# Making a key tile's scores in place from its neighbour's, with the keys' difference, in an attention and mixture-of-experts kernel

## The chip, the cores and the metric

The kernel runs on one core of a Trainium2 chip. The metric is the device time of one execution in microseconds (us); lower is better. A core has TensorE (PE, matmuls), VectorE (DVE), ScalarE (ACT), GpSimd (POOL) and SyncE (SP), each with an instruction queue of its own that it works off in order. They wait for each other by semaphores. Matmuls write into PSUM, which here is eight banks of 128 x 512 float32; the other data lie in SBUF, and DMA queues move data between SBUF and the chip's memory (DRAM).

## The reference

One pre-norm layer on x of 8 x 1024 x 256, float32: `x + attention(layernorm(x))`, then `x + experts(layernorm(x))`. The attention has 16 heads of 16 dimensions and uses one projection for both keys and values:

```python
q, kv = split(x @ Wq), split(x @ Wkv)             # b*H, n, 16
q, kv = rotary(q) * SCALE, rotary(kv)
att = einsum('bmd,bnd->bmn', q, kv)               # 1024 x 1024 per head
out = einsum('bij,bjd->bid', softmax(att), kv)
return out @ Wout + bout
```

The expert part scores every token against 8 experts; each expert takes the 1024 tokens that score highest for it, normalises them, applies a two-layer GELU network, weighs the result and adds it to the tokens' rows.

## The kernel before

**Tiling of the attention.** The work is cut into 32 groups `i`: a batch element b of 8 and four heads. A group has two halves of 512 queries and eight tiles of 128 keys. One *step* handles one key tile for one half and all four heads, so a group has 16 steps and the attention 512. In a step the four heads make two pairs, and for each pair `step_pair` (line 381) issues this on PE:

- `row_max` for the first head (L329): queries times 512 keys into one bank of the pool `ps_m`, and a DVE reduction (L336) to the row's maximum. This runs 13 steps (`LEAD`) ahead of the scores.
- `score_pass` for both heads (L371): the scores, keys on the partitions, into a two-bank tile of the pool `ps_e`. The 64 contraction rows of a head hold its 16 dimensions four times: queries and keys are each split into a high part that fits the matmul's float32r format and a low rest, and the products of all four combinations are summed.
- `score_pass` again for both heads with `last` (L371, `ones_r`): a matmul with ones adds the negative row maxima, which lie in `top_bufs`, to the same tile. So every key tile's scores are finished by two passes per head.
- one exponential on ACT over the pair's 128 x 1024 scores (L397), into SBUF.
- `row_max` for the second head.

After both pairs, every even step issues the value matmuls of the two steps before it (`weigh_values`, L416): their result is copied out of a `ps_m` bank by ACT (L429) and added up on POOL (L431). After every eighth step's maxima, `lay_max` (line 340) combines them on DVE, transposes them on PE and has SP write them to `top_bufs` with eight small DMAs (L363); the first steps of the next half need these.

**Buffers that tie engines together.** `ps_m` has four banks, given out in program order to maxima tiles, value sums, projections, transposes. `ps_e` has two tiles, one for each pair in turn, so each pair gets the same tile in every step. The work pool `side` has two buffers per tag, `prob` six, `kq` three for keys and four for queries.

**Work beside it.** Two kinds of generators are advanced piece by piece between steps by `run_pieces` (line 566): the *prologue* of the next batch element (layer norm, projections L280, rotation on POOL L203 to L206, transposes, splits) and the *epilogue* of the last (output projection L492, two layer norms, gate scores). A piece with much PE work is only taken after an odd step, one per step. In the prologue `split_halves` (line 212) copies a transposed block out of PSUM on ACT as `full` (L222), makes its high part `hi` and its rest `lo` on POOL (L223, L224), and SP writes each to DRAM, twice (L231). Each batch element has eight such calls in four pieces: two halves of its 256 columns, two halves of its tokens, query and key. Groups are loaded from there by `load_keys` and `load_queries` on SP (L304, L315), when the list `loads` (lines 588 to 599) says so: keys of group i from step 16(i-2) on.

**Order.** The tile framework is told to keep the program's order (`manual_schedule`), so each engine's queue is in the order in which these Python functions issue. For the first batch element the prologue runs before the steps, and the first step's maxima follow its loads.

**After the attention** come the selection of each expert's tokens, 30 rounds of bisection on DVE, and the experts' matmuls (from about 1845 us on). The change doesn't touch them.

Of the kernel before, what the change touches and what calls it, by code (L numbers as in the profile page):

```python
# [8 lines left out]
F32 = mybir.dt.float32  # L9
F32R = mybir.dt.float32r  # L10
# [16 lines left out]
def preln_attention_moe_kernel(  # L27
# [50 lines left out]
    with ExitStack() as actx:  # L78
# [132 lines left out]

        def split_halves(b, hf, c, s, pt):

            q_d, k_d = halves[b]
            hi = side.tile([P, QW], F32R, tag="hi", name="hi")
            lo = side.tile([P, QW], F32R, tag="lo", name="lo")
            if b == 0 and c == 0:
                nc.scalar.copy(hi, pt)
                nc.vector.tensor_tensor(lo, pt, hi.bitcast(F32), ALU.subtract)
            else:  # L220
                full = side.tile([P, QW], F32, tag="full", name="full")
                nc.scalar.copy(full, pt)  # L222
                nc.gpsimd.tensor_copy(hi, full)  # L223
                nc.gpsimd.tensor_tensor(lo, full, hi.bitcast(F32), ALU.subtract)  # L224
            rows = slice(c * P, (c + 1) * P)
            for part, src_t in enumerate((hi, lo)):
                if s == 0:
                    dst = q_d[hf, rows, 2 * part : 2 * part + 2, :]
                else:
                    dst = k_d[rows, part::2, hf * QW : (hf + 1) * QW]  # L230
                nc.sync.dma_start(dst, src_t.bitcast(F32).unsqueeze(1).to_broadcast([P, 2, QW]))  # L231
# [8 lines left out]
        def prologue(b):  # L240
# [3 lines left out]
            halves[b] = (q_d, k_d)  # L244
# [5 lines left out]
            qks, xns = [], []  # L250

            def normalised(hf):
                stats = yield from row_stats(xts[hf], "a")
                xn = side.tile([P, T2, D], F32, tag="n", name=f"xn_{b}_{hf}")
                scaled(nc.vector if b == 0 else nc.gpsimd, xn, xts[hf], stats)
                xns.append(xn)
# [3 lines left out]
            for hf in range(2):  # L260
                yield "x"
                xnT = one.tile([P, DC, QW], F32, tag="T", name=f"xnT_{b}_{hf}")
                for c in range(DC):
                    pt = transposed(lambda t: xns[hf][:, t, c * P : (c + 1) * P])
                    nc.scalar.copy(xnT[:, c, :], pt)
# [22 lines left out]
            for c in range(DC):  # L288
                for hf in range(2):
# [3 lines left out]
                    for s in range(2):  # L293
                        pt = transposed(lambda j: qks[hf][:, j, s, c * P : (c + 1) * P])
                        split_halves(b, hf, c, s, pt)
                ready[(b, c)] = True

        def load_keys(i):

            b, g = divmod(i, NG)  # L300
            k = kq.tile([P, 2, N], F32R, tag="k", name=f"k_{i}")
# [6 lines left out]
            grp[i] = {"k": k, "q": []}  # L308

# [58 lines left out]
        def score_pass(i, half, kt, h, last, pt):  # L368
            k, q = grp[i]["k"], grp[i]["q"][half]
# [7 lines left out]
                start=not last,  # L377
                stop=last,
            )

        def step_pair(pair, max_job, exp_job):
# [7 lines left out]
            pt = ps_e.tile([P, 2, QW], F32, tag="e", name="ps_s")  # L389
# [4 lines left out]
            score_pass(*exp_job, e1, True, pt)  # L394
            score_pass(*exp_job, e0, True, pt)
# [168 lines left out]
        ready = {}  # L564
# [22 lines left out]

        loads = []
        for i in range(B * NG):
            needs = (i // NG, i % NG // (NG // DC))  # L590
            loads.append((16 * (i - 2) if i > 2 else -(10**6), needs, load_keys, (i,)))
# [376 lines left out]
```

## Time and profile before

| | |
|---|---|
| median of 3 runs | 2510.09 us (2509.98 to 2511.71) |
| the profiled execution | 2509.83 us, span 2508.1 us |
| mean granted PE clock | 0.946 |
| busy in the span: PE, DVE, ACT, POOL | 2235.2, 1738.8, 1361.3, 1154.8 us |
| steps begin with maxima only / with scores / attention ends | 53 / 87 / about 1845 us |
| DMA | 207.5 MB, mean 83 GB/s |

A profile line of a group of instructions reads: source line, engine, operation, output<-input, shapes, count | busy us, mean ns of one | idle us of that engine just before them, and who ended most of it. A timeline line reads: start us, us, engine, line, operation, tiles, shapes, count of instructions merged, and in brackets the idle time ahead of it with the releaser. In a line of the windows stand a stretch from:to and its length, then busy us (and instructions) of PE, its weight loads, DVE, ACT and POOL, then the granted PE clock (1 is full), the mean busy share of the 16 DMA engines and GB/s. Matmuls on different rows of the array overlap, so the busy times of PE's groups add up to more than its total.

### The profile page before, as it was taken

To read this page: it belongs to the slowest core of one execution; us is meant where nothing else is said; L and a number is where in the kernel's file an instruction comes from. 1 tells how busy PE (TensorE), PEld (TensorE's weight loads), DVE (VectorE), ACT (ScalarE), POOL (GpSimd) and SP (SyncE) were. 2 spreads that over 40 slices of the span, in tenths; PEclk is the share of its full clock that TensorE was granted. 3 is DMA by queue.
4 is the path that set the end of the run, shared out by engine and by line. 5 is a ranking of instruction groups with operands and counts; after the bars stand their busy time and mean duration, and the time that the engine had idled before them with its cause. 6 is when DMAs were issued, how large, how long until landed. Compare 5 with 4: busy or idle time off the path is not lost. (4 is left out here: it accounts for less than half of the span.)

```text
span 2508.1 us, 38250 instructions
## 1 busy us (share of the span) xinstructions
PE 2235.2 (89%) x14228; PEld 1228.0 (49%) x14228; DVE 1738.8 (69%) x3303; ACT 1361.3 (54%) x1723; POOL 1154.8 (46%) x1060
## 2 busy tenths in 40 slices
PE   4999999999999999999999999999952289999998
PEld 2444444445444444444444544445431146666665
DVE  5978878888888788779778878888646843331111
ACT  1477777677677667767766777677720011111111
POOL 3274276456446744654674475344220044443332
PEclk8799999999999999999999999999975589999999
DMA  5215115212331412142142215121030013333321
GB/s 186 92 35 194 61 35 194 68 52 102 128 102 35 177 65 73 69 161 86 52 157 81 75 54 179 52 69 52 27 110 9 1 30 85 74 69 70 77 45 28
DMA packets 127210, 207.50 MB, mean 83 GB/s; under 512 B 13360, under 2 KB 65456, under 8 KB 126896
## 3 DMA queue, kind: packets, MB, share of 16 engines
q1 hardware_dynamic: 113616, 186.39, 21.7%
q0 software_dynamic: 12288, 17.05, 4.1%
q8 instruction: 113, 1.85, 0.3%
q10 hardware_dynamic: 1120, 1.61, 0.2%
q14 instruction: 73, 0.60, 0.1%
HBM read 111.42 MB, written 92.54 MB: 81 GB/s over the span
## 5 line engine op out<-in xcount | busy, mean ns | idle before, releaser
L336 DVE TENSOR_REDUCE nm<-ps_x 128x1 f32<-128x512 f32 x2048 | 1266.9, 681 | 256.7 <-PE ps_x L329 252.2
L397 ACT ACTIVATE e<-ps_s 128x1024 f32<-128x1024 f32 x1024 | 997.0, 1025 | 183.6 <-PE ps_x L329 162.7
L329 PE MATMUL ps_x<-k,q 64*128 64x512 f32 x2048 | 790.6, 435 | 48.3 <-ACT full L222 23.1
L371 PE MATMUL ps_s<-q,k 64*128 64x512 f32 x2048 | 677.8, 432 | 11.4 <-ACT e L397 11.0
L371 PE MATMUL ps_s<-top,ones_r 64*128 64x512 f32 x2048 | 609.6, 394 | 0.0
L329 PEld LDWEIGHTS ps_x<-k,q 64*128 64x128 f32 x2048 | 373.9, 188 | 411.8 <-DVE nm L336 238.2
L416 PE MATMUL ps_av<-e,v 128*32 128x512 f32 x4096 | 504.4, 611 | 16.9 <-DVE nm L336 16.4
L431 POOL TENSOR_TENSOR av<-av,avp 128x512 f32<-128x512 f32 x191 | 244.5, 1280 | 554.9 <-ACT avp L429 554.8
L371 PEld LDWEIGHTS ps_s<-top,ones_r 64*128 64x128 f32 x2048 | 362.3, 187 | 38.0
L371 PEld LDWEIGHTS ps_s<-q,k 64*128 64x128 f32 x2048 | 314.0, 186 | 64.8 <-ACT e L397 47.2
L879 ACT ACTIVATE hT<-ps_h,b 128x512 f32<-128x512 f32 x128 | 88.0, 687 | 369.9 <-PE ps_h L872 369.9
L894 DVE TENSOR_TENSOR o<-ps_o,b2b 128x256 f32<-128x256 f32 x64 | 27.2, 425 | 357.3 <-PE ps_o L886 357.3
L896 POOL DMA_INDIRECT out<-o,idx x64 | 127.4, 1991 | 282.1 <-DMA out<-o,idx 135.2
L416 PEld LDWEIGHTS ps_av<-e,v 128*32 128x32 f32 x4096 | 108.5, 110 | 266.4 <-issue 173.8
L872 PE MATMUL ps_h<-yT,w 128*128 128x512 f32 x512 | 226.4, 600 | 7.7 <-DVE yT L860 7.5
L886 PE MATMUL ps_o<-w,hT 128*128 128x256 f32 x1024 | 223.6, 379 | 0.0
L886 PEld LDWEIGHTS ps_o<-w,hT 128*128 128x128 f32 x1024 | 194.6, 190 | 33.3 <-issue 7.7
L429 ACT COPY avp<-ps_av 128x512 f32<-128x512 f32 x192 | 112.7, 587 | 176.3 <-PE ps_av L416 169.3
L872 PEld LDWEIGHTS ps_h<-yT,w 128*128 128x128 f32 x512 | 96.9, 192 | 125.7 <-issue 109.8
L844 POOL DMA_INDIRECT g<-rows_d,idx x64 | 70.5, 1102 | 148.0 <-DVE ids L819 128.8
L280 PE MATMUL ps_p<-wqkv,xnT 128*128 128x512 f32 x256 | 126.1, 619 | 2.5 <-DVE nm L336 2.2
L203 POOL TENSOR_TENSOR u<-pe,sin 128x256 f32<-128x256 f32 x112 | 79.2, 728 | 84.1 <-ACT pe L197 84.1
(137 smaller groups left out, 1862.8 us busy)
## 6 DMA issues: line engine op xcount, KB each, us to landing
k<-k_d SPq DMA_DIRECT2D x64, 512.0 KB
q<-q_d SPq DMA_DIRECT2D x128, 256.0 KB
q_d<-hi SPq DMA_DIRECT2D x32, 512.0 KB
q_d<-lo SPq DMA_DIRECT2D x32, 512.0 KB
k_d<-hi SPq DMA_DIRECT2D x32, 512.0 KB
k_d<-lo SPq DMA_DIRECT2D x32, 512.0 KB
w<-in_fc_t SPq DMA_DIRECT2D x16, 1024.0 KB
rows_d<-rows SPq DMA_DIRECT2D x16, 528.0 KB
```

What stands on the lines that cost most here:

```text
L280: nc.tensor.matmul(pp, lhsT=xnT[:, c, j * P : (j + 1) * P], rhs=wqkv[:, c].rearrange("p a d -> p (a d)"), start=(c == 0), stop=(c == DC - 1),)
L329: nc.tensor.matmul(pt, lhsT=q[r : r + 64, h // 2, j * P : (j + 1) * P], rhs=k[r : r + 64, h // 2, kh * QW : (kh + 1) * QW], start=True, st ...
L336: nc.vector.tensor_reduce(grp[i]["nm"][:, kh, h, j : j + 1], pt, AX.X, ALU.max, negate=True)
L371: nc.tensor.matmul(pt[:, h % 2, :], lhsT=ones_r[r : r + 64, :] if last else k[r : r + 64, pair, kt * P : (kt + 1) * P], rhs=(top_bufs[half ...
L397: nc.scalar.activation(e.rearrange("p h q -> p (h q)"), pt.rearrange("p h q -> p (h q)"), AF.Exp, scale=DH**-0.5,)
L416: nc.tensor.matmul(pa[HS * h : HS * (h + 1), :], lhsT=v_bufs[b % 2][:, kt, c : c + HS], rhs=es[h // 2][:, h % 2, :], start=(n == 0), stop= ...
L429: nc.scalar.copy(part, pa)
L431: (nc.vector if end else nc.gpsimd).tensor_tensor(av, av, part, ALU.add)
L872: nc.tensor.matmul(ph, lhsT=w1[:, c, f * P : (f + 1) * P], rhs=yT[:, c, :], start=(c == 0), stop=(c == DC - 1),)
L879: nc.scalar.activation(hT[:, f, :], ph, AF.Gelu_apprx_tanh, bias=b1[:, e * FC + f : e * FC + f + 1])
L886: nc.tensor.matmul(po, lhsT=hT[:, f, j * P : (j + 1) * P], rhs=w2[:, f, :], start=(f == 0), stop=(f == FC - 1),)
L896: nc.gpsimd.indirect_dma_start(out=out_rows[:, :], out_offset=bass.IndirectOffsetOnAxis(ap=idx[:, t : t + 1], axis=0), in_=o, in_offset=No ...
```

## The change

The scores of one key tile are q times k of that tile, less the maxima. Those of the next key tile differ from them by q times the difference of the keys, position by position. The changed kernel keeps a pair's PSUM tile over four key tiles: for the first of four it makes the scores as before, with the pass that subtracts the maxima; for the next three it only adds q times the keys' difference to what stands in the tile, and takes the exponential again. For this the prologue makes, of every block of keys, the differences (the first tile of each four stays whole), splits them into high part and rest like the keys, and writes them to a third DRAM tensor; a load per group brings them into SBUF. The maxima (`row_max`) still use the keys themselves.

Further: the layer-normed x is written over x; keys get two buffers for three, and are loaded later; the differences have two buffers; an additional condition finishes the prologue if a group's differences are not yet loaded.

```diff
+        def write_halves(d, rows, cols, hi, lo, keys):
+            for part, src_t in enumerate((hi, lo)):
+                pair = slice(part, None, 2) if keys else slice(2 * part, 2 * part + 2)
+                nc.sync.dma_start(
+                    d[rows, pair, cols], src_t.bitcast(F32).unsqueeze(1).to_broadcast([P, 2, QW])
+                )
         def split_halves(b, hf, c, s, pt):
...
-            if b == 0 and c == 0:
+            full = None
+            if first:
                 nc.scalar.copy(hi, pt)
                 nc.vector.tensor_tensor(lo, pt, hi.bitcast(F32), ALU.subtract)
-            else:
+            if not first or s == 1:
                 full = side.tile([P, QW], F32, tag="full", name="full")
                 nc.scalar.copy(full, pt)
+            if not first:
                 nc.gpsimd.tensor_copy(hi, full)
                 nc.gpsimd.tensor_tensor(lo, full, hi.bitcast(F32), ALU.subtract)
...
+            return full
+
+        def split_steps(b, hf, c, full):
+            dif = side.tile([P, QW], F32, tag="u", name="dif")
+            nc.gpsimd.tensor_copy(dif[:, 0:P], full[:, 0:P])
+            nc.gpsimd.tensor_tensor(dif[:, P:QW], full[:, P:QW], full[:, 0 : QW - P], ALU.subtract)
+            hi = side.tile([P, QW], F32R, tag="hi", name="dhi")
+            lo = side.tile([P, QW], F32R, tag="lo", name="dlo")
+            nc.gpsimd.tensor_copy(hi, dif)
+            nc.gpsimd.tensor_tensor(lo, dif, hi.bitcast(F32), ALU.subtract)
+            write_halves(
+                halves[b][2], slice(c * P, (c + 1) * P), slice(hf * QW, (hf + 1) * QW), hi, lo, True
+            )
...
-                xn = side.tile([P, T2, D], F32, tag="n", name=f"xn_{b}_{hf}")
-                scaled(nc.vector if b == 0 else nc.gpsimd, xn, xts[hf], stats)
-                xns.append(xn)
+                scaled(nc.vector if b == 0 else nc.gpsimd, xts[hf], xts[hf], stats)
...
             for c in range(DC):
+                fulls = []
                 for hf in range(2):
...
                     for s in range(2):
                         pt = transposed(lambda j: qks[hf][:, j, s, c * P : (c + 1) * P])
-                        split_halves(b, hf, c, s, pt)
+                        full = split_halves(b, hf, c, s, pt)
+                    if b > 0 or c > 0:
+                        yield "s"
+                        split_steps(b, hf, c, full)
+                    fulls.append(full)
                 ready[(b, c)] = True
+                if b == 0 and c == 0:
+                    for hf in range(2):
+                        yield "s"
+                        split_steps(b, hf, c, fulls[hf])
+                steps_ready[(b, c)] = True
...
-            k = kq.tile([P, 2, N], F32R, tag="k", name=f"k_{i}")
+            k = kq.tile([P, 2, N], F32R, tag="k", name=f"k_{i}", bufs=2)
...
+        def load_steps(i):
+            b, g = divmod(i, NG)
+            k = kq.tile([P, 2, N], F32R, tag="s", name=f"s_{i}", bufs=2)
+            for pair in range(2):
+                d0 = DH * (4 * g + 2 * pair)
+                nc.sync.dma_start(
+                    k.bitcast(F32)[:, pair, :],
+                    halves[b][2][d0 : d0 + 2 * DH].rearrange("d j n -> (d j) n"),
+                )
+            grp[i]["steps"] = k
...
         def score_pass(i, half, kt, h, last, pt):
-            k, q = grp[i]["k"], grp[i]["q"][half]
+            k, q = grp[i]["steps"], grp[i]["q"][half]
...
-                start=not last,
-                stop=last,
-            )
+                start=not last and kt % T2 == 0,
+                stop=last or kt % T2 != 0,
+                skip_group_check=True,
+            )
...
-            pt = ps_e.tile([P, 2, QW], F32, tag="e", name="ps_s")
+            first = exp_job[2] % T2 == 0
+            if first:
+                score_tiles[pair] = ps_e.tile([P, 2, QW], F32, tag="e", name="ps_s")
+            pt = score_tiles[pair]
             if max_job is not None:
                 row_max(*max_job, e0)
             score_pass(*exp_job, e1, False, pt)
             score_pass(*exp_job, e0, False, pt)
-            score_pass(*exp_job, e1, True, pt)
-            score_pass(*exp_job, e0, True, pt)
+            if first:
+                score_pass(*exp_job, e1, True, pt)
+                score_pass(*exp_job, e0, True, pt)
...
-            loads.append((16 * (i - 2) if i > 2 else -(10**6), needs, load_keys, (i,)))
+            loads.append((16 * (i - 1) - LEAD + 1 if i > 1 else early, 0, ready, needs, load_keys, (i,)))
+            loads.append((16 * (i - 1) + 1 if i > 1 else early + 1, 2, steps_ready, needs, load_steps, (i,)))
...
-            if with_max and mstep == 0 and mi not in grp:
+            if with_max and mstep == 0 and mi not in grp or with_exp and "steps" not in grp[i]:
                 finish(starts)
                 run_loads(s)
```

## The prediction

> **What bounds the kernel now.** I read the table of slices first: TensorE (PE) is 9 tenths busy from about 95 to 1840 us, the attention. Then the groups:
>
> ```profile
> L336 DVE TENSOR_REDUCE nm<-ps_x 128x1 f32<-128x512 f32 x2048 | 1266.9, 681 | 256.7 <-PE ps_x L329 252.2
> L397 ACT ACTIVATE e<-ps_s 128x1024 f32<-128x1024 f32 x1024 | 997.0, 1025 | 183.6 <-PE ps_x L329 162.7
> L371 PE MATMUL ps_s<-q,k 64*128 64x512 f32 x2048 | 677.8, 432 | 11.4 <-ACT e L397 11.0
> L371 PE MATMUL ps_s<-top,ones_r 64*128 64x512 f32 x2048 | 609.6, 394 | 0.0
> ```
>
> VectorE (DVE) and ScalarE (ACT) idle for PE, so PE leads, narrowly: DVE is busy 186 of 224 us in each 64-step batch. What a matmul costs shows in the timeline of PE, then of DVE:
>
> ```profile
> 1017.21 0.49 PE L329 MATMUL ps_x<-k,q 64*128 64x512 f32 x1
> 1017.55 0.62 PE L371 MATMUL ps_s<-top,ones_r 64*128 64x512 f32 x2
> ...
> 1018.48 0.39 PE L329 MATMUL ps_x<-k,q 64*128 64x512 f32 x1
> 1018.79 1.98 PE L280 MATMUL ps_p<-wqkv,xnT 128*128 128x512 f32 x4
> 1020.71 0.49 PE L329 MATMUL ps_x<-k,q 64*128 64x512 f32 x1
> ```
>
> ```profile
> 1017.74 2.48 DVE L336 TENSOR_REDUCE nm<-ps_x 128x1 f32<-128x512 f32 x4 [1.09 <-PE ps_x L329]
> 1021.24 2.48 DVE L336 TENSOR_REDUCE nm<-ps_x 128x1 f32<-128x512 f32 x4 [1.01 <-PE ps_x L329]
> ```
>
> A step's twelve 64-row matmuls start 0.115 us apart (1.27/11), the next group 0.31 later; then an even step has the value matmuls (1.86, from 1015.36 to 1017.21), an odd one sometimes a projection (1.92). So even 3.44, odd with projection 3.50. Odd steps without side work are ACT-bound: four exponentials in a row (3.88 at 109.21) and two steps take 5.80.
>
> The batch repeats every 224 us, and in six batches this stands at its end (timelines of POOL and ACT, then the windows):
>
> ```profile
> 1069.28 4.84 POOL L175 TENSOR_SCALAR xf<-xr,mv_b,rs_b 128x256 f32<-128x256 f32 x4
> 1074.20 2.39 POOL L505 TENSOR_TENSOR xr<-xr,xf 128x1024 f32<-128x1024 f32 x1
> 1076.55 1.29 POOL L431 TENSOR_TENSOR av<-av,avp 128x512 f32<-128x512 f32 x1
> ```
>
> ```profile
> 1070.16 1.08 ACT L222 COPY full<-ps_t 128x512 f32<-128x512 f32 x2
> ...
> 1079.77 0.59 ACT L222 COPY full<-ps_t 128x512 f32<-128x512 f32 x1 [2.78 <-POOL lo L224]
> 1081.68 0.59 ACT L222 COPY full<-ps_t 128x512 f32<-128x512 f32 x1 [1.33 <-POOL lo L224]
> ```
>
> ```profile
> 1082.00:1084.00 2.00, 1.68 (x9) 0.58 (x13) 0.69 (x1) 2.00 (x3) 1.92 (x3) 0.50 1.02 386
> ```
>
> GpSimd (POOL) is late with split work behind layer-norm work; ACT, in order, waits with a copy; the exponentials queue behind it; PE idles, and its clock falls to 0.50 for some 6 us. That pair of steps takes 10.9 us and the next 8.7, where 6.3 each is usual: 7 us.
>
> **What the Trainium skill says.** "TensorE: Matmul & The Clock Gate", Part 3, The mechanism: matmuls on different row groups overlap; the 0.115 us agrees. Same page, Part 1, What's actually happening: an idle window of about 3.4 us halves the clock; the 0.50 agrees. "DMA: Bandwidth & Descriptors", Anatomy of one DMA: about 2 us fixed beside the bytes; here a 512 KB write issued at 33.72 frees its buffer at 36.6, later ones take 4. "SBUF — State Buffer", two separate sides: DVE and GpSimd lock each other out of a shared port; a small DVE operation of 0.17 takes 1.15 at 1031.5.
>
> **The change, part by part.** *Removed:* both ones passes in three of four steps: 4 matmuls x 0.115 = 0.46 us a step, 384 steps, 177 us of PE. It doesn't pass through. The next group in a step takes the PSUM buffer of the step's first maxima tile: DVE starts 0.53 after that matmul, needs 0.68, and PE sees it 0.06 later: 1.27. PE would be there at 0.81 + 0.31 = 1.12, where it was at 1.58. So a changed step saves 0.30, not 0.46. The first of each four key tiles is always an even step: half the even steps keep their passes and save nothing, all odd steps are changed. A pair of steps without side work falls from 5.80 to 5.54: there the value matmuls waited for the last scores, these for the exponentials (1.07 after the first matmul, two of 0.97); without the passes the exponentials start 0.25 earlier, and DVE binds (0.53, five reductions 0.60 apart: 3.08, 0.06, 1.86).
> Where DVE has other work in its gap (statistics 1.17, the laying of maxima 0.6 to 2, residual adds 0.69) nothing is saved: the gap must stay 0.66 long (1.86 + 0.53 + 0.06, less three reductions, 1.80, rounded). Going through DVE's gaps of the batch 859 to 1083: six give 0.3, three give 0.5 together, eight pairs without projection 0.25 each: 4.3 us. Times 6.65 batches (93 to 1636, less 227 to 281) 28.6. Light stretches: nine pairs (227 to 281) 2.3, 27 pairs (1636 to 1800) 6.2, six pairs without maxima 1.4. Sum 38.5 us; bounds 20 (port locks eat the gaps) and 60 (gaps overlap better).
> *In-place scores:* no new wait. Each pair already got the same one of the two PSUM buffers every step, so its scores waited for the exponential of the step before as they will now.
> *Added on POOL:* per piece a 128x128 copy (0.25, estimated from 0.40 for 128x256), a 128x384 subtraction (0.98, from 1.28), a cast 0.61 and a subtraction 1.28: 3.1 us, 32 times, 100 us on 1154.8. Hidden behind PE except where the buffers tie in: `full` has two, and the key half must now also outlive the difference. In program order this stands behind the 8.5 us of layer norm and the value add. So the second copy of the third split, made at 1070.7 now, waits for 1077.8 + 1.2 = 1079.0: 8.3 us on ACT, with the exponentials behind it and the value matmuls behind those. These come at 1080.1 for 1072.1, at half clock. The fourth split's copy waits for the third's difference, itself behind two DMA round trips (`hi` and `lo`, two buffers each, now taken three times a piece): about 1088.7. The value matmuls after it come at 1089.7 for 1083.0: 6.7 late, of which the 2.4 lost now to the clock right after are already paid: 4.3 net, six times, 26 us. In the batch without an epilogue (200 to 222) POOL needs 8.2 us a piece where a pair takes 6.3: 2 us. Bounds for all this: 15 (the stall only replaces the old one and DVE catches up) and 60 (slow round trips).
> *Start:* the writes of the differences (SyncE's queue, SP) wait for POOL, which waits for earlier writes; SP has the eight writes of the first maxima behind them. They were issued at 75.7; chaining the round trips (4 us each) I get 85, so the first ones pass at 91.7 instead of 88.1: 3.5 us (0 to 8).
> *DMA:* 64 writes and 64 loads of 512 KB, 67 MB on 207.5. Loads of keys come 28 steps ahead of their scores and 15 before their maxima, differences 15 steps (50 us) before use; landing takes about 5: hidden. Without that cover each would cost its 5 us. In the split windows the engines are full (share 1.02), which is in the round trips.
> *Normalising in place, one key buffer less:* nothing; PE has long released them. ACT's two extra copies at the start (0.59) fall in its idle time.
>
> Sum, against the profiled run (2509.83, span 2508.1; median of the runs 2510.09): 2509.8 - 38.5 + 26 + 2 + 3.5 = 2503.
>
> **Rivals.** *The stall is cheap* (0.25): while ACT waits, DVE finishes its statistics and catches up, or the gaps give more. For it: DVE runs without a gap from 1069 to 1079. Against: it has nothing to reduce while PE is stopped. Time 2509.8 - 38.5 = 2471 and up to 2490; all 177 us (2333) are excluded by the 2.48 us of DVE in every step.
> *POOL decides* (0.30), the other side: in the split window each reuse of `hi` and `lo` waits for a DMA, and with the engines at 1.02 a round trip of 6 us instead of 4 adds 2 us at two places, and SP's maxima behind the last difference come up to 2 us late, PE waiting at its next ones pass. 26 becomes 26 + 6 x 5 = 56: 2535. It decides above 5.5 us net a batch (38.5 less 5.5, over six).
> *DVE is already the bound, nothing moves* (inside 0.45 with the forecast): DVE's continuous stretches speak for it, its gaps of 1.0 against; time 2510 + 5.
>
> **The numbers.** Forecast case, both effects as computed, 0.45: 2503, own range 2490 to 2517. Fast rival 0.25: 2450 to 2490; slow rival 0.30: 2517 to 2555. Range 2468 to 2545 leaves out about 0.15. A measurement tells about 0.2% (2505 to 2515) from no change: of the forecast case half is faster, 0.35 within, the rest slower; so faster 0.47, same 0.18, slower 0.35.
>
> **What would show it.** Right: 512 ones matmuls; a middle batch whose ordinary stretch is some 4 us shorter; DVE gaps of 0.66 to 0.8 after value matmuls; pairs of 5.55 us; one wait of 8 us of ACT's `full` copy on POOL per batch, six times, with a clock of 0.50; SP's first maxima near 85 us. Wrong: no such wait, or one with two or three more behind it; even steps of first tiles getting shorter, or pairs without side work still at 5.80.

## The result and the profile after

| | median | runs | profiled execution, span | granted clock |
|---|---|---|---|---|
| before | 2510.24 us | 2509.98 to 2511.71 | 2509.83, 2508.1 us | 0.946 |
| after | 2546.49 us | 2541.93 to 2548.84 | 2548.73, 2547.0 us | 0.925 |

The changed kernel is slower: ratio 1.0141, 95% interval 1.0123 to 1.0159. The forecast was 2503, its range ended at 2545. What was to get shorter did, by nearly what was forecast when it is read pair by pair; the cost was forecast at 31.5 us and comes to about 76 in the same reading (below).

The groups of the changed kernel, the same as were shown of the kernel before:

```profile
L381 DVE TENSOR_REDUCE nm<-ps_x 128x1 f32<-128x512 f32 x2048 | 1266.5, 682 | 289.6 <-PE ps_x L374 288.5
L451 ACT ACTIVATE e<-ps_s 128x1024 f32<-128x1024 f32 x1024 | 998.6, 1026 | 149.7 <-PE ps_x L374 77.4
L374 PE MATMUL ps_x<-k,q 64*128 64x512 f32 x2048 | 753.7, 461 | 89.0 <-ACT full L232 47.5
L418 PE MATMUL ps_s<-top,ones_r 64*128 64x512 f32 x512 | 157.6, 411 | 12.9 <-DMA top<-mrows 12.8
```

The ones passes fell from 2048 to 512, VectorE and ScalarE do what they did. New are the last fields of the PE rows: PE waited 47.5 us for ScalarE's copies `full` (22.0 before, from 95 to 1840 us) and 12.8 for the rows of maxima, 6.8 of these at the start and 6.0 in the batches (none before).

Away from the ends of batches, the timeline of PE and VectorE shows what the forecast said: the step at 1035.24 has its eight passes and no ones passes, and VectorE's gap after value matmuls (at 1039.60) is 0.66.

```profile
1035.24 0.49 PE L374 MATMUL ps_x<-k,q 64*128 64x512 f32 x1
1035.25 0.72 PE L418 MATMUL ps_s<-q,s 64*128 64x512 f32 x2
...
1039.60 1.93 PE L470 MATMUL ps_av<-e,v 128*32 128x512 f32 x16
```

```profile
1038.85 2.48 DVE L381 TENSOR_REDUCE nm<-ps_x 128x1 f32<-128x512 f32 x4
1041.99 0.69 DVE L381 TENSOR_REDUCE nm<-ps_x 128x1 f32<-128x512 f32 x1 [0.66 <-PE ps_x L374]
```

**The long wait.** The timelines of GpSimd and ScalarE at the end of the fourth batch's window of splits (some 21 us later than the lines shown of before):

```profile
1093.52 4.84 POOL L175 TENSOR_SCALAR xf<-xr,mv_b,rs_b 128x256 f32<-128x256 f32 x4
1098.44 2.34 POOL L559 TENSOR_TENSOR xr<-xr,xf 128x1024 f32<-128x1024 f32 x1
1100.74 1.26 POOL L485 TENSOR_TENSOR av<-av,avp 128x512 f32<-128x512 f32 x1
...
1102.19 0.99 POOL L248 TENSOR_TENSOR dif<-full 128x384 f32<-128x384 f32 x1
```

```profile
1103.22 0.58 ACT L232 COPY full<-ps_t 128x512 f32<-128x512 f32 x1 [8.46 <-POOL dif L248]
```

ScalarE waits 8.46 us for the difference that stands behind the layer norm: the wait of the forecast, six times.

**Where the time went, pair by pair.** I took the start of every group of value matmuls (one per two steps, 256 in each kernel) from both timelines and compared the spacing of each with that of the same pair before. What follows the last of them takes 675.7 us for 675.4, so nearly all of the difference lies in these spacings and in the start of the first.

| part | us | forecast |
|---|---|---|
| all pairs not named below, net (-44.4 in those that got shorter, +7.6 in those that got longer) | -36.8 | -38.5 |
| first value matmuls at 102.19 for 93.89 | +8.3 | +3.5 |
| six long waits (14.9 for 6.7 each), less the two shorter pairs after each | +29.7 | +26 |
| batch without epilogue (a pair at 228) | +5.9 | +2 |
| residual's addition meets the laying of the maxima (pairs at 455, 1145, 1375: 5.4, 5.3, 4.1) | +14.8 | none |
| PE waits longer for the laying of the maxima, and its clock falls (pairs at 179, 821, 1053: 1.9 each) | +5.8 | none |
| pairs in which the first pass with the maxima waits for their rows, or behind them (seven, most at 901 and 910, 1591 and 1607) | +11.0 | none |
| after the last value matmuls | +0.3 | none |
| sum | +38.9 | -7 |

The largest part that the forecast lacks looks like this; timelines of VectorE, GpSimd and PE at 457 us:

```profile
456.80 2.29 DVE L389 TENSOR_TENSOR both<-nm 128x16 f32<-128x16 f32 x1
459.12 1.19 DVE L391 CAST parts<-both 128x16 fp32r<-128x16 f32 x1
```

```profile
456.65 2.40 POOL L525 TENSOR_TENSOR xr<-xr,bo 128x1024 f32<-128x1024 f32 x1 [9.56 <-DMA xr<-in_x]
459.00 1.28 POOL L485 TENSOR_TENSOR av<-av,avp 128x512 f32<-128x512 f32 x1
```

```profile
461.17 0.39 PE L397 MATMUL ps_l<-ident,parts 128*32 128x128 f32 x1 [2.57 <-DVE nm L381]
461.77 3.78 PE L546 MATMUL ps_o<-wo,aoT 128*128 128x256 f32 x8 [0.20 <-DVE nm L381]
```

VectorE's operations on 128x16 take 0.17 us where GpSimd is idle. Here the first lasts as long as GpSimd's addition of the bias to the residual, the second as long as the next addition. The Trainium skill, "SBUF — State Buffer", Who interferes with whom, has the rule: a VectorE instruction with two SBUF inputs and a GpSimd instruction that reads SBUF exclude each other, a cast (the second operation) can when it runs in a mode that uses both ports, while a reduction is not concerned. The trace agrees: the 863 reductions that run wholly beside GpSimd's work take 0.68 us on average, as the others do. PE, in order, waits with the transpose of the maxima for 2.57 us, its clock falls (0.50 from 462 to 466 us), and the projection behind it takes 3.78 for 1.99. In the kernel before the same addition ran at 439.65, 5.7 us ahead of that batch's laying at 445.35.

The three pairs of 1.9 us are another matter. There the laying runs during GpSimd's rotation, as it did before, with the same two operations of 0.57 and 1.13 us (0.58 and 1.15 before) in all seven batches. But PE comes to the transpose earlier without the ones passes, and waits longer. The timelines of PE, before and after:

```profile
1033.33 0.28 PE L352 MATMUL ps_l<-ident,parts 128*32 128x128 f32 x1 [0.58 <-DVE nm L336]
1033.93 1.98 PE L280 MATMUL ps_p<-wqkv,xnT 128*128 128x512 f32 x4 [0.32 <-DVE nm L336]
```

```profile
1056.94 0.28 PE L397 MATMUL ps_l<-ident,parts 128*32 128x128 f32 x1 [1.25 <-DVE nm L381]
1057.54 3.12 PE L303 MATMUL ps_p<-wqkv,xnT 128*128 128x512 f32 x4 [0.31 <-DVE nm L381]
```

PE waits 1.25 or 1.26 us in all seven batches. In three of them the clock then falls to 0.50 and the projection takes 3.1 to 3.7 us; in the other four it takes 1.98 and the pair loses 0.3 us. What decides between the two wasn't found.

### The profile page after: what moved, and what is told of

The parts are those of the page before. It is cut to its first block, busy times and chain, and to the rows that moved or that the text cites. A ratio compares the mean times of both kernels' runs of the same rounds, so it can differ in the third digit from the quotient of the medians.

```text
span 2547.0 us, 35507 instructions
## 1 busy us (share of the span) xinstructions
PE 2165.2 (85%) x12692; PEld 1154.6 (45%) x12692; DVE 1745.9 (69%) x3303; ACT 1363.5 (54%) x1725; POOL 1251.5 (49%) x1188
## 5 line engine op out<-in xcount | busy, mean ns | idle before, releaser
L374 PE MATMUL ps_x<-k,q 64*128 64x512 f32 x2048 | 753.7, 461 | 89.0 <-ACT full L232 47.5
L418 PE MATMUL ps_s<-q,s 64*128 64x512 f32 x2048 | 643.2, 435 | 13.6 <-ACT e L451 10.5
L374 PEld LDWEIGHTS ps_x<-k,q 64*128 64x128 f32 x2048 | 363.3, 191 | 495.8 <-DVE nm L381 304.8
L470 PE MATMUL ps_av<-e,v 128*32 128x512 f32 x4096 | 511.1, 618 | 29.2 <-DVE nm L381 24.8
L418 PEld LDWEIGHTS ps_s<-q,s 64*128 64x128 f32 x2048 | 320.6, 188 | 53.2 <-ACT e L451 35.6
L418 PE MATMUL ps_s<-top,ones_r 64*128 64x512 f32 x512 | 157.6, 411 | 12.9 <-DMA top<-mrows 12.8
L303 PE MATMUL ps_p<-wqkv,xnT 128*128 128x512 f32 x256 | 131.7, 643 | 4.8 <-DVE nm L381 4.4
L418 PEld LDWEIGHTS ps_s<-top,ones_r 64*128 64x128 f32 x512 | 94.6, 194 | 26.4 <-DMA top<-mrows 13.7
```

The lines of the kernel that those rows point to most:

```text
L303: nc.tensor.matmul(pp, lhsT=xnT[:, c, j * P : (j + 1) * P], rhs=wqkv[:, c].rearrange("p a d -> p (a d)"), start=(c == 0), stop=(c == DC - 1),)
L374: nc.tensor.matmul(pt, lhsT=q[r : r + 64, h // 2, j * P : (j + 1) * P], rhs=k[r : r + 64, h // 2, kh * QW : (kh + 1) * QW], start=True, st ...
L418: nc.tensor.matmul(pt[:, h % 2, :], lhsT=ones_r[r : r + 64, :] if last else k[r : r + 64, pair, kt * P : (kt + 1) * P], rhs=(top_bufs[half ...
L470: nc.tensor.matmul(pa[HS * h : HS * (h + 1), :], lhsT=v_bufs[b % 2][:, kt, c : c + HS], rhs=es[h // 2][:, h % 2, :], start=(n == 0), stop= ...
```

## The experiments

Each is timed beside the kernel before on its own chip (medians there 2510.6 to 2512.2).

| run | median, us | ratio to before |
|---|---|---|
| gain_only | 2481.56 | 0.9883 (0.9865 to 0.9901) |
| all_passes | 2567.53 | 1.0222 (1.0205 to 1.0239) |
| full4 | 2546.52 | 1.0133 (1.0117 to 1.0150) |
| late_loads | 2550.82 | 1.0150 (1.0125 to 1.0175) |
| no_pool_work | 2498.25 | 0.9956 (0.9939 to 0.9972) |
| residual_in_eight | 2536.18 | 1.0112 (1.0092 to 1.0131) |
| splits_alone | 2532.44 | 1.0092 (1.0075 to 1.0108) |
| before_splits_alone | 2502.23 | 0.9963 (0.9949 to 0.9977) |
| halves3 | 2532.82 | 1.0090 (1.0073 to 1.0107) |
| alone_full4 | 2472.82 | 0.9847 (0.9830 to 0.9863) |
| second_half_late | 2477.98 | 0.9863 (0.9847 to 0.9879) |
| alone_late_full4 | 2475.43 | 0.9853 (0.9836 to 0.9869) |
| before_alone_full4 | 2519.60 | 1.0035 (1.0026 to 1.0045) |
| alone_full4_b | 2469.56 | 0.9831 (0.9814 to 0.9847) |
| late_only | 2481.56 | 0.9879 (0.9863 to 0.9896) |
| order_full4 | 2475.96 | 0.9864 (0.9848 to 0.9881) |
| before_order_full4 | 2516.94 | 1.0022 (1.0007 to 1.0037) |

### The gain and the cost, each alone

gain_only, in the kernel before:

```diff
-                stop=last,
+                stop=last or kt % T2 != 0,
...
-            score_pass(*exp_job, e1, True, pt)
-            score_pass(*exp_job, e0, True, pt)
+            if exp_job[2] % T2 == 0:
+                score_pass(*exp_job, e1, True, pt)
+                score_pass(*exp_job, e0, True, pt)
```

> The kernel before with one thing done: the maxima are subtracted only at the first of each four key tiles. The scores still come from the keys, one new sum a tile, so three of four tiles go without their maxima (that part of the computation is left out); no differences are made, written or loaded. Theory A (the change has two additive halves, a gain of 40 us read from the pairs that got shorter in the changed kernel, and about 79 us of costs in separate places): 2510 - 40 = 2470 us, range 2462 to 2478. Theory B (the skipped passes gain little, and the shorter pairs of the changed kernel are pairs that catch up after a stall): 2490 to 2510. In my prediction this was 38.5 us: 2471.

all_passes, in the changed kernel:

```diff
-            if first:
+            if True:
                 score_pass(*exp_job, e1, True, pt)
```

> The changed kernel with both passes of the maxima in every step again (so maxima are subtracted up to four times: that part of the computation is altered). The differences, their writes and loads and the order of the loads are all kept. Theory A (additive): before + 79 = 2589 us, range 2575 to 2600. Theory B (the costs come only because PE runs faster and has less slack for late rows and port locks): the costs shrink with the passes back, 2520 to 2560.

The missing passes alone are worth 29 us (25 to 34 by the interval), not 40. By pairs, 53 us got shorter, but 22 came back, 7.7 of them in four pairs (at 348, 570, 1229, 1451): there PE waits 1.26 us for the laying of the maxima and its clock falls, as in the three pairs above. The added work alone costs 56 us (51 to 60), not 79; its trace has the same six pairs of 14.9. Both times lie between the ranges of the two theories. Summed, 2511 - 29 + 56 = 2538, and the changed kernel measures 2546: 8 us above the sum, about what the intervals allow together. So gain and cost are both real and nearly additive, and theory A was too high on both.

### Two cures that don't cure

full4, in the changed kernel:

```diff
-                full = side.tile([P, QW], F32, tag="full", name="full")
+                full = side.tile([P, QW], F32, tag="full", name="full", bufs=4)
...
-            rows = side.tile([P, T2, ROW], F32, tag="rows", name=f"rows_{b}_{hf}")
+            rows = side.tile([P, T2, ROW], F32, tag="rows", name=f"rows_{b}_{hf}", bufs=1)
```

> The changed kernel with four buffers for the copies in full precision (full) in place of two, and one in place of two for the rows that the epilogue writes, to make room. Theory A (ScalarE's copy that waits 8 us for the difference is one of several places, 31 us net of the 79, and the old wait of about 7 us an end of batch, which the kernel before has too, may go with it): 2546 - 31 = 2515 us, range 2485 to 2520; late residuals and late maxima rows stay. Theory C (GpSimd's added work as a whole sets the time, and what no longer waits on the copy waits on the split keys, the writes or the maxima rows instead): 2535 to 2550.

The six pairs of 14.9 are gone (6.2 now), and the time is the same (1.0133 of the kernel before, where the changed kernel has 1.0141). In the seven pairs that follow each of them 6 to 15 us more are lost than in the changed kernel: at 411 to 437, 652 to 683, 872 to 897 and so on. No wait for the single `rows` buffer stands in this trace. The timelines of PE and GpSimd in this run show the new place:

```profile
662.50 1.12 PE L496 MATMUL ps_d<-ident,av 128*128 128x128 f32 x4 [7.46 <-POOL av L485]
```

```profile
656.36 4.85 POOL L175 TENSOR_SCALAR rows<-xf,mv_c,rs_c 128x256 f32<-128x256 f32 x4
661.18 1.27 POOL L485 TENSOR_TENSOR av<-av,avp 128x512 f32<-128x512 f32 x1
```

ScalarE is hardly held any longer (13.4 us in six waits, 2.3 at most), but GpSimd is as late as it was. The addition of the value sums stands in its queue behind the epilogue's second layer norm (`rows`, 27 us after the one that held the copy in the changed kernel), and PE, in order, stops at the transposes of those sums: 36.1 us in seven waits, six of them behind this layer norm. Theory A falls, theory C holds: the copy's wait was only the first door at which GpSimd's lateness came out.

late_loads, in the changed kernel:

```diff
-            loads.append((16 * (i - 1) - LEAD + 1 if i > 1 else early, 0, ready, needs, load_keys, (i,)))
-            loads.append((16 * (i - 1) + 1 if i > 1 else early + 1, 2, steps_ready, needs, load_steps, (i,)))
+            loads.append((16 * (i - 1) - LEAD + 5 if i > 1 else early, 0, ready, needs, load_keys, (i,)))
+            loads.append((16 * (i - 1) + 4 if i > 1 else early + 1, 2, steps_ready, needs, load_steps, (i,)))
```

> The changed kernel with only two due times moved: the keys of the next group are loaded four steps later, and its differences three steps later, so that on SyncE's queue they come after the maxima rows (top) and away from the residual's load. Same work, same bytes. Theory A (rows of maxima behind the loads of the differences cost 11 us, and the residual that lands late, whose addition on GpSimd then meets VectorE's laying of the maxima, 15 us): 2546 - 26 = 2520 us, range 2510 to 2535; the six waits of 8 us of ScalarE's copy stay. Theory C (GpSimd's added work sets the time, the place of the loads does not matter): 2543 to 2550.

No gain. The waits for the rows of maxima in the batches did go, from 6.0 us to none. But the residual still met the laying of the maxima, at other places (687 and 1738, where an operation of 0.17 takes 2.35 and 2.28), and ScalarE's waits from 95 to 1840 us grew from 63.3 to 68.4 us. Moving these loads moves the collisions and doesn't remove them.

### What of the cost is GpSimd's work

no_pool_work, in the changed kernel (`split_halves` also returns its halves, and the first two pieces write those of the second half of the tokens):

```diff
-            dif = side.tile([P, QW], F32, tag="u", name="dif")
-            nc.gpsimd.tensor_copy(dif[:, 0:P], full[:, 0:P])
-            nc.gpsimd.tensor_tensor(dif[:, P:QW], full[:, P:QW], full[:, 0 : QW - P], ALU.subtract)
-            hi = side.tile([P, QW], F32R, tag="hi", name="dhi")
-            lo = side.tile([P, QW], F32R, tag="lo", name="dlo")
-            nc.gpsimd.tensor_copy(hi, dif)
-            nc.gpsimd.tensor_tensor(lo, dif, hi.bitcast(F32), ALU.subtract)
+            _, hi, lo = full
```

> The changed kernel without the arithmetic of the differences on GpSimd: the halves of the keys are written in their place to the differences' scratch (so three of four tiles add up products with keys, not with differences: that part of the computation is altered). All DMAs, their bytes and their order on SyncE's queue stay, and so do the missing passes. Theory C (GpSimd's 100 us of added work, 12.4 us of it in one window a batch where GpSimd is behind already, is the whole cost beyond the start): 2482 of the run with the gain alone + some 5 at the start = 2487 us, range 2478 to 2500. Theory D (the 67 MB of writes and loads, the longer round trips and the loads ahead of the maxima rows on SyncE's queue are the cost): 2520 to 2547. In between says how it is shared.

2498: of the 65 us between the gain alone (2481.6) and the changed kernel (2546.5), 48 go with GpSimd's arithmetic; 17 stay with the DMAs, their order and the copies, 6.4 of these at the start. The run also leaves out the third taking of the buffers `hi` and `lo` in each piece, so the 48 hold the waits for these as well; halves3 below bears on that. Theory C has the larger part.

residual_in_eight, in the changed kernel:

```diff
-                nc.gpsimd.tensor_tensor(xt, xt, bo.unsqueeze(1).to_broadcast([P, T2, D]), ALU.add)
+                for t in range(T2):
+                    for c in range(DC):
+                        cs = slice(c * P, (c + 1) * P)
+                        nc.gpsimd.tensor_tensor(xt[:, t, cs], xt[:, t, cs], bo[:, cs], ALU.add)
```

> The changed kernel with one edit: the addition on GpSimd that puts the output bias to the residual is issued as eight instructions of 128x128 in place of one of 128x1024. Theory P (VectorE's three small operations of laying the maxima are locked out for as long as one GpSimd instruction lasts; in three batches this one of 2.4 us costs 4 to 5 us each, 14.8 us in all): each locked operation waits 0.3 us in place of 2.1, and some 10 of the 14.8 us come back: 2546 - 10 = 2536 us, range 2530 to 2541. Rival (the lock is not what costs there, the late landing of the residual is, or GpSimd keeps the port from one instruction to the next): 2543 to 2551.

10 us came back by the medians, as theory P said (7 by the ratios, whose intervals overlap). The trace shows where: the three pairs named got all of their 5.4, 5.3 and 4.1 back, and the rest of it adds up to less than 1. The residual lands as late as it did and meets the same operations, timelines of VectorE and GpSimd:

```profile
456.31 0.21 DVE L389 TENSOR_TENSOR both<-nm 128x16 f32<-128x16 f32 x1
456.56 0.38 DVE L391 CAST parts<-both 128x16 fp32r<-128x16 f32 x1
456.97 0.38 DVE L392 TENSOR_TENSOR parts<-both,parts 128x16 fp32r<-128x16 f32 x1
```

```profile
455.19 3.37 POOL L528 TENSOR_TENSOR xr<-xr,bo 128x128 f32<-128x128 f32 x8 [11.02 <-DMA xr<-in_x]
```

Each of them now ends 0.03 us after one of eight short instructions. That the lock-out is what costs in these three pairs is shown.

splits_alone, in the changed kernel, and before_splits_alone, the same in the kernel before:

```diff
                 first = tasks is not urgent
+                if tasks is ends and starts and 22 <= s % (2 * T * NG) <= 32:
+                    continue
```

> The changed kernel with one edit: between steps 22 and 32 of a batch, where the next batch's queries and keys are split and the differences made, the pieces of the epilogue wait. Its layer norms (4.84 us on GpSimd each) come after the splits in GpSimd's order and not between them. Same work, same buffers. Theory C (GpSimd's backlog in that window costs 31 us net in the changed kernel, and the old stall of 7 us a batch has the same root): 2546 - 30 to 60 = 2486 to 2516 us; ScalarE's copy waits under 2 us on the difference. Rival (the backlog moves on, as with four buffers, and stops TensorE at the transposes of the value sums or at the maxima rows): 2538 to 2552.

> The kernel before with the same edit of the order: the epilogue's pieces wait between steps 22 and 32 of a batch. Theory C (the stall that the kernel before has at this place, 7 us in six batches, comes from GpSimd's layer norm between the splits): 2511 - 20 to 40 = 2470 to 2491 us. Rival (the stall is DMA round trips of hi and lo, or it moves with the layer norm to a later place): 2505 to 2515.

Both gained less than expected: 14 and 9 us. In the changed kernel ScalarE's copies still wait 31.8 us for differences (from 95 to 1840 us), 5.1 at most, now with no layer norm ahead of them: the copies have only two buffers, and GpSimd waits for `hi` and `lo` of the differences (13.7 and 6.7 us), the first of whose writes stand behind SyncE's eight rows of maxima. And the epilogue, ten steps later, reached the end of the batch, where its last pieces are issued at once; the pairs at 744 and 969, for instance, lost 3.8 and 4.3 us.

### Buffers and order together

halves3 gives the tags `hi` and `lo` three buffers (`bufs=3` in four places, and one for `rows` as in full4).

> The changed kernel with three buffers in place of two for the halves hi and lo (and one in place of two for the rows that the epilogue writes, to make room). Theory C (GpSimd's own work in the window of the splits is the cost): 2541 to 2549 us, the 8 us waits of ScalarE's copy stay. Theory D (GpSimd is held there by the DMA that still reads a half, in which case my slow rival's round trips would be the cause): 2515 to 2535.

Between the theories: 13 us back, though the waits of the copies are all there (the list of waits of this run):

```profile
ACT full L232 <- POOL dif L248: 55.0, 7, 8.5
```

What came back is spread: 3.8 at the start, 2.6 in the batch without an epilogue (1.5 of it lost again in the next pair), the rest in small steps; of three pairs with late rows of maxima (8.3 us) most went to others (6.7 at 900 and 1586). So the DMA round trips cost, but not where the long wait is.

alone_full4, in the changed kernel: the edits of splits_alone, full4 and residual_in_eight, the epilogue's last pieces until step 8, and the first differences loaded later:

```diff
-            if s > 0 and g == 0 and step == 0:
+            if s > 0 and g == 0 and step == 8:
...
-            loads.append((16 * (i - 1) + 1 if i > 1 else early + 1, 2, steps_ready, needs, load_steps, (i,)))
+            loads.append((16 * (i - 1) + 1 if i > 1 else -4, 2, steps_ready, needs, load_steps, (i,)))
```

> The changed kernel with the layer norms out of the window of the splits (epilogue's pieces wait in steps 22 to 32 of a batch, and its last pieces may run until step 8 of the next batch), four buffers for the full copies, the bias added in eight instructions, and the first two groups' differences loaded after the first maxima rows. Theory C: GpSimd is behind by only the 12.4 us of differences in the window, four buffers take that up, 2546 - 14 (order) - 10 (eight instructions) - 25 (the waits that are left) - 4 (start) = 2493 us, range 2483 to 2512. Rival (backlog of any size stops TensorE at the transposes of the value sums, as with four buffers alone): 2515 to 2530.

second_half_late, in the changed kernel: full4, residual_in_eight, the later first loads, and

```diff
-                    if b > 0 or c > 0:
+                    if b > 0 and c == 0:
                         yield "s"
                         split_steps(b, hf, c, full)
...
+                if c == 1:
+                    yield 6
+                    for hf in range(2):
+                        yield 2
+                        split_steps(b, hf, c, fulls[hf])
                 steps_ready[(b, c)] = True
```

> The changed kernel with the differences of the second half of the dimensions (c = 1, two of four pieces) made 6 to 10 steps after the splits, four buffers for the full copies, the bias in eight instructions and the first loads of differences after the first maxima rows. The epilogue stays where it was. Theory C (half of the 12.4 us leave the window): 2546 - 10 - 4 - half of the 48 us that GpSimd's arithmetic costs = 2508 us, range 2498 to 2520. Rival (the backlog in the window is the layer norms, moving differences helps little): 2525 to 2536.

alone_late_full4 has the edits of both:

> Both orders together: epilogue's pieces out of the window of the splits and the second half's differences 6 to 10 steps later; four buffers for the full copies, the bias in eight instructions, the first loads of differences after the first maxima rows. Theory C: GpSimd keeps up in the window, and what is left over the 2482 us of the gain alone is DMA and order, some 10 us: 2490 us, range 2478 to 2505. Rival (differences and epilogue now meet in the steps after): 2505 to 2525.

All three land at 2473 to 2478, 15 to 30 us below what the separate gains sum to, and both orders together bring no more than one. Four buffers alone brought nothing and the order alone 14; together, with the smaller edits, they brought some 70. The next two runs leave out two of the smaller edits.

late_only is second_half_late without the eight instructions and the later first loads; order_full4 is alone_full4 without these two.

> second_half_late without the bias in eight instructions and without the later first loads: the changed kernel with four full buffers, one rows buffer, and the second half's differences 6 to 10 steps later. If the collisions at the residual and the late maxima rows follow from the backlog: some 2482 us (2478 of second_half_late and 4 of the start). If they are causes of their own: 2478 + 10 + 4 = 2492 us or more.

> alone_full4 without the bias in eight instructions and without the later first loads. If the collisions follow from the backlog: 2473 + 4 = 2477 us. If they are causes of their own: 2473 + 14 = 2487 us. If the later flush alone made the difference to splits_alone and the four buffers nothing, this can't tell them apart; the waits of ScalarE's copy in its trace do.

2482 and 2476: the two smaller edits bring little. The times are those expected if the collisions and the late rows follow from the backlog, but each trace bears out only one half of that. In late_only no pass waits for rows of maxima, but the residual still meets the laying in three batches (pairs at 872, 1317, 1539, which lose 4.2, 3.1 and 3.2 us against the kernel before); the first value matmuls, at 94.27 for 102.19, make up for most of it. Timeline of VectorE:

```profile
873.97 2.36 DVE L396 CAST parts<-both 128x16 fp32r<-128x16 f32 x1
```

In order_full4 the residual is added after the laying, but PE waits 5.6 us for rows in the batches, for 6.0 in the changed kernel. The waits on GpSimd do get less: from 95 to 1840 us PE waits for the value sums 17.3 us in late_only and 3.7 us in order_full4, in place of the 36.1 of full4, and no wait of ScalarE's copies on the difference is left in order_full4:

```profile
PE ps_d L496 <- POOL av L485: 3.7, 1, 3.7
```

So it is enough that half of the differences or the layer norms leave the window, with ScalarE tied to GpSimd by four buffers. The two differences are 6.2 us of GpSimd's work; the layer norms with their statistics and the addition are 8.5 and 6.1. Whether the four buffers are needed for this is not shown: no run moves the differences with two buffers, and splits_alone differs from order_full4 also in when the epilogue's last pieces are issued.

Is it then the change that pays, or the order? alone_full4_b repeats alone_full4 beside the kernel before with the same edits (without the loads of differences); before_order_full4 is that kernel with the bias in one instruction.

> The kernel before with the order and buffers of alone_full4: epilogue's pieces out of the window of the splits, its last pieces until step 8 of the next batch, four full buffers, one rows buffer, the bias in eight instructions. All passes, no differences. If the gain of alone_full4 is the order's and not the passes': 2475 to 2485 us. If the skipped passes are worth their 30 us with the old stall gone too: 2472 + 30 - 5 at the start = 2497 us, range 2490 to 2503.

> alone_full4 once more, on the chip of before_alone_full4: 2471 to 2475 us.

> The kernel before with the order and buffers of order_full4 (epilogue's pieces out of the window of the splits, its last pieces until step 8 of the next batch, four full buffers, one rows buffer), the bias added in one instruction as before. If the long lock-out of before_alone_full4 (about 8 us in four batches, 30 us) came with the eight short instructions: 2520 - 30 = 2490 us, range 2483 to 2500, and order_full4 (2476) is then 10 to 20 us faster by the missing passes. If it comes with the place of the addition in the order and not with its pieces: 2505 to 2522.

This order helps only the changed kernel: 2476 and 2470 against 2517 and 2520. So the order alone is not the gain. Neither expectation for before_alone_full4 came: the kernel before loses something else under this order, from 7 to 8 us in each of four batches in one trace and in two of them in the other, at single operations of VectorE that take 5.94 and 4.96 us (below). The bias's eight pieces, suspected first, are not their cause: they come with one instruction too. So the 41 to 50 us are not all the passes'. An estimate from the spans of these traces: without the long operations (7 us each, the difference of the same pairs in the two traces) the kernel before would take 2494 to 2497 for 2472 of order_full4 and alone_full4, so the passes would be worth 22 to 25 us there. Of the orders tried, the kernel before is fastest with that of before_splits_alone (2502), 26 to 33 us above the changed kernel's 2470 and 2476.

## Why the prediction was wrong

*Removed.* Right as a sum of the pairs: 36.8 net for 38.5, with most pairs without side work at 5.52 to 5.56 (forecast 5.54), gaps of 0.66, a step without ones passes 1.29 long. Measured alone it is 29, within the bounds of 20 and 60. The forecast named the lock of VectorE during the rotation and its 1.15 us, but only as something that eats gaps. It missed that PE, faster than before, then waits 1.25 us at the transpose for 0.58, and that its clock can fall after that.

*In-place scores.* No wait of their own, as said: nothing in the pairs away from the windows.

*Added on POOL, 26 us.* The wait was placed and priced rightly: 8.46 for 8.3, six times, 5.0 net each for 4.3. The step that failed is the end of that sum: it took the wait as what GpSimd's lateness costs. GpSimd's arithmetic with its waits for buffers cost 48 us, and full4 showed that the wait could be removed with nothing gained. The clause "Hidden behind PE except where the buffers tie in" is the wrong one. The value sums, the split keys, the writes and through SyncE's queue the rows of maxima stand behind GpSimd's work, and late_only and order_full4 showed that 65 to 70 us come back once 6 us of differences, or some 15 of layer norms, leave the window and the copies have four buffers. What the lateness meets next was worked out for one queue, ScalarE's; it was needed for GpSimd's own.

*Batch without epilogue.* 5.9 for 2: ScalarE's copy waits 5.2 us for the difference here too.

*Start.* 8.3 for 3.5. The first maxima's rows were issued at 90.28 for the forecast 85: SyncE also had the loads of the first differences ahead of them, and waited with these until 67.42 for the writes to land. With those loads behind the rows and the second half's differences late, the first value matmuls come at 95.97 (second_half_late); with these differences late and the loads where they were they come at 94.27 (late_only). So the two pieces of differences and their writes are the larger part, not the loads' place.

*DMA: "hidden".* Not wholly: 17 us of the cost stay without GpSimd's arithmetic, and only the 6.4 at the start have a place. In the batches the rows of maxima stand in SyncE's queue behind the differences' writes and loads. The timeline of SyncE in the changed kernel, and from its waits from 885 to 912 us the longest:

```profile
899.55 1.50 SPq L349 DMA_DIRECT2D s<-s_d  x2
901.14 6.84 SPq L408 DMA_DIRECT2D top<-mrows  x8
```

```profile
SPq L216 <- POOL dhi L251: 6.5, 1, 6.5
```

ScalarE had copied these rows by 893.84. The loads ahead of them held SyncE for 1.50 us; 6.5 us were the write ahead of the loads, which waited for GpSimd's difference behind its layer norm. So here too it is GpSimd's lateness that comes out.

*The rivals.* "POOL decides" had the right sign, and its rows up to 2 us late were there, PE waiting 6.0 us for them in the batches. Its main part, round trips of 2 us at two places before the long wait, was not: halves3 left the wait at 8.5. That its span of 2517 to 2555 holds the result is luck: each case priced one mechanism, and the collisions were in none. Its sum is also off by two (26 and 30 in place of 26 give 2533 and not 2535), and the shares of the cases give 0.16 for the same and 0.37 for slower, not 0.18 and 0.35; neither changes the argument.

## What to carry to other kernels

When work is added to an engine that is already late at one place, price all that stands behind it in that engine's queue, not only the wait that ends last now; a wait can be removed and the time stay, because the next reader of the same late engine takes it over. First give the late engine less to do in that window and loosen the buffers there, then judge the change: as made it cost 1.4%, with the epilogue's pieces moved by ten steps and four buffers in place of two it is 1.4% faster than the kernel before, and up to 1.7% with the smaller edits. And look at where small operations on VectorE meet long ones on GpSimd, since in front of a PE transpose 3 us of waiting there became 4 to 5.

## What the runs showed of the hardware

The lock-out can last longer than one GpSimd instruction. In before_alone_full4, timelines of VectorE and GpSimd:

```profile
771.51 5.94 DVE L347 TENSOR_TENSOR parts<-both,parts 128x16 fp32r<-128x16 f32 x1
```

```profile
771.48 1.29 POOL L431 TENSOR_TENSOR av<-av,avp 128x512 f32<-128x512 f32 x1
772.73 3.33 POOL L474 TENSOR_TENSOR xr<-xr,bo 128x128 f32<-128x128 f32 x8
776.02 1.39 POOL L203 TENSOR_TENSOR u<-pe,sin 128x256 f32<-128x256 f32 x2
777.49 1.26 POOL L205 TENSOR_TENSOR pe<-pe,cos 128x512 f32<-128x512 f32 x1
```

An operation that takes 0.17 us alone ended at 777.45, after eleven GpSimd instructions without a gap, in the first gap (0.08). The page of the Trainium skill named above says that the instruction that starts first holds the shared pair of ports to its end and the other waits; it does not say which gets the pair between two instructions that follow each other closely. Here the wait lasted for eleven. In residual_in_eight, eight instructions as close let VectorE in after one.

What decides between the two no run tried. The traces show one difference. In all six long cases (four here, two in before_order_full4) VectorE's operation began 0.02 to 0.03 us after GpSimd's addition of the value sums had begun, with 0.06 us of the copy ahead of it still to run. In the two other batches of before_order_full4 it began with 0.12 us of that copy to run, ahead of the addition, and took 1.38 us; in order_full4 and alone_full4 it is so in all four batches (1.35 or 1.36). So under this order some 0.07 us in when the operation begins go with 7 us of a batch's time.
